# Fetching two feature rows per sample by DMA instead of turning them on TensorE, in a fused four-stage residual kernel

## The chip, the cores and the metric

The kernel runs on one core of a Trainium2 chip. The metric is the device time of one execution in microseconds (us), from three runs of the kernel before and, beside it, one execution taken with the hardware profiler. Engines are named as in the profile: PE is TensorE's matrix multiply, PEld its weight load, DVE is VectorE, ACT is ScalarE, POOL is GpSimd, SP is SyncE, which here only issues DMAs.

## What is computed

There are B = 128 samples, each a block of S = 128 positions by D = 512 features in float32. Four stages follow each other, and each adds its result to its input:

```
x1 = x  + pooled(softmax over a masked score, per sample one of three masks) / count
x2 = x1 + layernorm(x1 + relu(x1 @ W1[lang] + b1) @ W2[lang] + b2) * gamma[lang] + beta[lang]
x3 = x2 + zX * lap_x(x2) + zY * lap_y(x2) + zR * x2 * (1 - x2)
out = x3 + x3 @ W3[cat] + b3[cat]
```

`lap_x(y)` at a feature is left neighbour - 2y + right neighbour along the features; `lap_y` is the same along the positions. At both ends the neighbour is reflected: left of feature 0 stands feature 1, right of feature 511 stands feature 510. zX, zY and zR are one number per sample. `lang` picks one of 10 tables, `cat` one of 64 weight matrices of 512x512.

The change concerns the third stage and what it hands to the fourth.

## The kernel before

**Stages over iterations.** One sample takes several iterations of a software pipeline. `plan` is a hand-written list of (offset, function) pairs; iteration i runs through it and calls each function for sample i + offset. The order of the calls is the order of the instructions on every engine (`tc.manual_schedule()`), and no engine overtakes. The first iterations are written out one call at a time in `ramp`, up to about sample 4; after that the plain plan runs. Each iteration therefore does every stage once, for different samples, and its length is the time per sample.

**What stands where.** For sample b = i: scores and softmax (offset 0). Offset -1: the pooled sum, `pooled`, and the weight load `category` (one DMA of 1 MB, `w3_b`). Offset -2: the adapter's second product (`adapter`, L444), the layer norm (`statistics` on ACT, `deviation` on POOL, `centred` and `norm` on DVE), `edges` on ACT, which writes the two reflected columns 0 and 513 of the tile `y`, and `residual` on POOL (L597), which adds the identity matrix to `w3_b` so that the product gives x3 + x3 @ W. Offset -3: the diffusion stage. Offset -4: the product with `w3_b`, in three calls (`project_first`, `project_middle`, `project_last`, L604). Offset -5: `finish` on DVE (L618), which adds the bias row loaded by `category_row`, and `store`.

**The diffusion stage.** It is computed with features on partitions, since the product needs x3 transposed. `y_transpose` (L524) does four TensorE transposes of 128x128, each taking every fourth feature, so that partition p holds features 4p to 4p+3 as four planes of 128 positions. Neighbours along the positions are then neighbours in a plane. Neighbours along the features are the plane before and the plane after, except for a partition's first and last feature: their outer neighbours, 4p-1 and 4p+4, stand on partitions p-1 and p+1. The kernel before gets these two from two more transposes (L528, tile `tr_e`, called `outer`). `planes` copies all of it from PSUM to one tile of six planes, `yT`, on ACT: the four inner planes (L534), the two outer ones (L535) and the two reflected positions (L536). POOL then adds the neighbours: `ud` along the positions (L549), `lr` along the features (L557). ACT computes `own` (L541), a linear function of y, and DVE finishes in three steps: y * own (L564), + zY * ud (L568), + zX * lr (L575), which gives `x3T`. The first two write back to the PSUM tile `tr_y`.

**Buffers.** `tr_y` has one PSUM buffer; the small PSUM tiles (`zh`, `sc`, `pTp`, `h1` and `tr_e`) share four in turn. `yT` has two buffers, `w3` four, the bias and output rows (`b`) four.

**Queues.** All DMAs of the loop are issued by SP, in the order of the plan: `category` (L582, 1 MB), `store` (L621), `category_row` (L588), four DMAs of `load_blocks` (L98, 64 KB each, pieces of 512 bytes), `load_x` (L84). ACT issues DMAs only at the start. Every DMA reports its completion on one of eight semaphores, which the framework hands out; a DMA that is given a semaphore first waits until the DMA that had it before has landed.

**In one iteration** PE runs, in this order: `adapter`, the four transposes `tr_y`, the two `tr_e`, the transpose `pTp`, the first quarter of the product `po`, the transpose `sc`, `pooled` and `h`, the other three quarters of `po`, and `zh` (`first_products`, L330). ACT runs: `hidden` (tanh, L348, and a copy, L350), the copy of `pTp` (L415), `planes`, `statistics` (L476), `exps`, `own`, `bank_bias` (L317), the two copies of `pooled_copy` (L427, L431), `first_weights` (L310) and `edges` (L512). POOL runs: `mean`, `ud`, `deviation`, `lr`, `with_beta` (L436), `residual` (L597).

Of the kernel before, what the change touches and what calls it, by code (L numbers as in the profile page):

```python
# [22 lines left out]
def kernel(  # L23
# [37 lines left out]
    w3p = ctx.enter_context(tc.tile_pool(name="w3p", bufs=4))  # L61
    blocks = ctx.enter_context(tc.tile_pool(name="blocks", bufs=3))
# [3 lines left out]
    ps_tr = ctx.enter_context(tc.tile_pool(name="ps_tr", bufs=1, space=PSUM))  # L66
    ps_sm = ctx.enter_context(tc.tile_pool(name="ps_sm", bufs=4, space=PSUM))
# [10 lines left out]
    EARLY = 8  # L78
    R = 32
# [109 lines left out]
    mid = one.tile([P, NC, S], F32, tag="own", name="mid_tile")  # L189
# [324 lines left out]
    def y_transpose(b):  # L514

        s = st[b]  # L520
        yp = s["yp"]
        s["yT"] = ps_tr.tile([P, NC, S], F32, tag="tr", name=f"tr_y_{b}")
        for c in range(NC):
            nc.tensor.transpose(s["yT"][:, c, :], yp[:, c + 1 : c + 2 + D - NC : NC], ident)  # L524
        s["outer"] = ps_sm.tile([P, 2, S], F32, tag="sm", name=f"tr_e_{b}")

        for i, at in ((1, NC + 1), (0, 0)):
            nc.tensor.transpose(s["outer"][:, i, :], yp[:, at : at + D - NC + 1 : NC], ident)  # L528

    def planes(b):  # L530
        s = st[b]
        s["planes"] = two.tile([P, NC + 2, S + 2], F32, tag="yT", name=f"yT_{b}")
        inner = s["planes"][:, 1 : NC + 1, :]
        nc.scalar.copy(inner[:, :, 1 : S + 1], s["yT"])  # L534
        nc.scalar.copy(s["planes"][:, 0 : NC + 2 : NC + 1, 1 : S + 1], s["outer"])  # L535
        nc.scalar.copy(inner[:, :, 0 : S + 2 : S + 1], inner[:, :, 2 : S : S - 3])  # L536

    def own(b):
        s = st[b]
        s["own"] = one.tile([P, NC, S], F32, tag="own", name=f"own_{b}")  # L540
        nc.scalar.activation(  # L541
            s["own"], s["yT"], AF.Identity, bias=column(cy, b), scale=column(nzr, b)
# [19 lines left out]
    def diffuse_own(b):  # L562
        s = st[b]
        nc.vector.tensor_mul(s["yT"], s["own"], s["yT"])  # L564

    def diffuse_rows(b):
        s = st[b]
        nc.vector.scalar_tensor_tensor(  # L568
            s["yT"], s["ud"], column(zy, b), s["yT"], ALU.mult, ALU.add
        )  # L570

    def diffuse_columns(b):
# [3 lines left out]
            s["x3T"], s["lr"], column(zx, b), s["yT"], ALU.mult, ALU.add  # L576
# [43 lines left out]
    def store(b):  # L620
# [6 lines left out]
        (-1, category),  # L627
        (-2, adapter),
        (0, hidden_bias),
        (-5, finish),  # L630
        (-5, store),
# [7 lines left out]
        (-4, project_first),  # L639
        (-2, adapter_bias),  # L640
        (-2, mean),
        (-3, planes),
        (-3, neighbours),
# [8 lines left out]
        (-4, project_middle),  # L652
        (-3, own),
        (-3, side_neighbours),
        (1, bank_bias),
        (-1, pe_index),
        (-4, project_last),
        (0, shares),
        (-3, diffuse_own),
        (-2, norm),  # L660
        (0, weights),
        (-3, diffuse_rows),
# [4 lines left out]
        (2, first_weights),  # L667
        (-2, edges),
        (-3, diffuse_columns),
        (1, mask_at),  # L670
        (-1, with_beta),
        (-2, residual),
        (-3, category_row),
# [8 lines left out]
        act_index.6 first_products.0 fetch_ids.0 pe_index.0 load_w2.0 load_w2.2 first_products.1  # L682
        load_x.3 fetch_b1.0 row_at.0 hidden_bias.0 hidden.0 row_at.1 row_at.2 row_at.3
        row_by.vb.0 early_weights.3 row_by.vo.1 score.0 row_by.ab.2 turn_first.2 load_w2.4
        row_by.ab.3 load_w2.6 hidden_bias.1 mask_at.0 row_by.ab.5 masked.0 row_by.ao.4 load_w2.8
        scores.0 category.0 row_by.ab.6 mask_at.1 least.0 mask_at.2 mask_at.3 row_by.ab.8
        mask_at.5 row_by.vb.7 load_x.4 mask_at.4 row_by.ao.9 row_by.ab.10 row_by.ao.11
        row_by.ab.12 fetch_factors.0 row_by.ao.13 exps.0 row_by.ab.14 category.1 early_weights.4
        shares.0 weights.0 row_by.ao.15 mix_transpose.0 row_by.vb.16 hidden.1 row_by.vb.17
        mix_copy.0 pooled.0 score.1 masked.1 row_by.vs.20 scores.1 row_by.as.18 pooled_copy.0  # L690
        row_by.ao.19 first_products.2 least.1 residual.0 load_x.5 exps.1 hidden_bias.2
        turn_first.3 row_by.vo.21 row_by.as.22 row_by.vs.23 hidden.2 early_weights.5 adapter.0
        shares.1 row_by.ao.26 load_w1.0 row_by.as.24 adapter_bias.0 mean.0 row_by.vs.25
        weights.1 turn_first.4 factors.0 row_by.vo.29 mix_transpose.1 mix_copy.1 statistics.0
        row_by.as.28 pooled.1 residual.1 row_by.ao.27 score.2 load_x.6 first_products.3 masked.2
        pooled_copy.1 deviation.0 hidden_bias.3 category.2 load_w1.1 with_beta.0 centred.0
        early_weights.6 adapter.1 adapter_bias.1 mean.1 with_beta.1 hidden.3 turn_first.5 norm.0
        load_x.7 first_products.4 edges.0 scores.2 least.2 y_transpose.0 statistics.1 exps.2
# [62 lines left out]
```

## Time and profile before

| | |
|---|---|
| median of three runs | 1078.42 us (1077.36 to 1078.7) |
| the profiled execution's own time | 1078.29 us |
| its span in the trace | 1076.4 us |
| PE, DVE, POOL, ACT busy | 1053.2, 885.9, 775.9, 666.3 us |
| granted TensorE clock, mean | 0.994 |
| moved by DMA | 275.97 MB, 256 GB/s |

The page of the profile gives, in this order, the busy time of each engine, the span in 40 slices, the DMA queues, the chain of work that ended last (followed back from the last instruction), the costliest groups of instructions and the DMA issues with the median time from issue to landing. The timeline lists instructions with their start and length in us; "x4" means four in a row, merged. Matmul ends are modelled, so the time that a matmul takes on PE is best read as the distance to the start of the next one. A float32 matmul counts as two.

### The profile page before, as it was taken

What the parts mean: (1) busy time and instruction counts of PE and PEld (TensorE: products, weight loads), DVE (VectorE), ACT (ScalarE), POOL (GpSimd) and SP (SyncE); (2) the same over time, 40 slices, a digit from 0 to 9 for tenths busy, and PEclk for the clock granted to TensorE, in tenths of its full rate; (3) what the DMA queues carried; (4) which work ended last, traced back from release to release, by engine and by line L of the source; (5) the groups of instructions that cost most, each with busy time, mean ns of one, the idle gap of its engine ahead of it and who ended that gap; (6) DMA issues with size and microseconds to landing.
All of it is one profiled execution on the core that took longest, in us unless ns stands there. A gap on an engine that the chain in (4) does not pass through costs nothing.

```text
span 1076.4 us, 19485 instructions
## 1 busy us (share of the span) xinstructions
PE 1053.2 (98%) x3966; PEld 642.8 (60%) x3966; DVE 885.9 (82%) x2070; ACT 666.3 (62%) x2062; POOL 775.9 (72%) x921
## 2 busy tenths in 40 slices
PE   6889999999999999999999999999999999999997
PEld 4655665666666666666656656656656666566653
DVE  3578888888888888888888888888888888888885
ACT  4656666566566566666666666666665665665652
POOL 2557777777777777777777777777777777777775
PEclk8999999999999999999999999999999999999999
DMA  8789888787787877887788887887877887878853
GB/s 290 213 218 315 254 277 260 254 273 258 259 271 254 266 267 250 269 268 249 269 268 249 271 266 248 272 268 247 277 260 253 273 256 263 270 252 265 267 185 115
DMA packets 152646, 275.97 MB, mean 256 GB/s; under 512 B 16689, under 2 KB 84532, under 8 KB 136146
## 3 DMA queue, kind: packets, MB, share of 16 engines
q1 hardware_dynamic: 152326, 274.60, 78.3%
q8 instruction: 35, 0.57, 0.2%
q14 instruction: 81, 0.66, 0.2%
q10 hardware_dynamic: 204, 0.13, 0.1%
HBM read 241.11 MB, written 33.55 MB: 255 GB/s over the span
## 4 chain that ended last, share of the span: by engine, by line
PE 95%; DVE 2%; ACT 1%; issue 1%; DMA 0%; POOL 0%; SPq 0%; DVEq 0%; POOLq 0%; ACTq 0%
PE po L604 40%; PE zh L330 21%; PE pool L420 10%; PE pool L444 10%; PE tr_y L524 6%; PE tr_e L528 3%; PE h L422 3%; PE pTp L410 1%; PE sc L380 1%; PE row L274 0%; DVE tr_y L568 0%; DVE x3T L575 0%; DMA x<-in_x_dram 0%; PE tr_x L291 0%; ACT b_tab L277 0%
## 5 line engine op out<-in xcount | busy, mean ns | idle before, releaser
L604 PE MATMUL po<-w,x3T 128*128 128x512 f32 x1024 | 482.4, 594 | 1.3 <-issue 1.3
L604 PEld LDWEIGHTS po<-w,x3T 128*128 128x128 f32 x1024 | 175.3, 191 | 126.3 <-issue 126.3
L330 PEld LDWEIGHTS zh<-w,xT 128*128 128x128 f32 x1088 | 199.7, 193 | 78.7 <-issue 29.9
L330 PE MATMUL zh<-w,xT 128*128 128x256 f32 (+1 forms) x1088 | 244.4, 370 | 0.9 <-ACT yT L535 0.9
L597 POOL TENSOR_TENSOR w<-w,ident 128x512 f32<-128x512 f32 x128 | 198.3, 1549 | 10.8 <-DMA w<-in_L_cond_W_dram 10.8
L549 POOL TENSOR_TENSOR ud<-yT 128x512 f32<-128x512 f32 x128 | 133.0, 1039 | 100.9 <-ACT yT L536 100.9
L348 ACT ACTIVATE zh<-zh 128x128 f32<-128x128 f32 x128 | 33.6, 262 | 219.3 <-PE zh L330 207.9
L436 POOL TENSOR_TENSOR x<-x,beta_tab 128x512 f32<-128x512 f32 x128 | 162.9, 1273 | 4.5 <-ACT x L431 3.5
L557 POOL TENSOR_TENSOR lr<-yT 128x512 f32<-128x512 f32 x128 | 163.8, 1280 | 0.0
L469 POOL TENSOR_SCALAR mean<-total 128x1 f32<-128x1 f32 x128 | 28.4, 222 | 147.1 <-DVE pool L456 138.1
L420 PE MATMUL pool<-x,pT 128*128 128x512 f32 x256 | 132.7, 600 | 0.8 <-DVE gamma_tab L277 0.4
L444 PE MATMUL pool<-w_tab,h1s 128*128 x256 | 130.8, 593 | 0.0
L415 ACT COPY pT<-pTp 128x128 f32<-128x128 f32 x128 | 34.0, 266 | 143.2 <-PE pTp L410 143.2
L524 PEld LDWEIGHTS tr_y<-ident,y 128*128 128x128 f32 x512 | 80.9, 204 | 66.2 <-issue 62.2
L494 DVE SCALAR_TENSOR_TENSOR pool<-pool,mean,gamma_tab 128x512 f32<-128x512 f32 x128 | 97.0, 758 | 25.4 <-ACT y L476 24.9
L385 DVE TENSOR_REDUCE least<-sc 128x1 f32<-128x128 f32 x128 | 37.3, 292 | 90.4 <-PE sc L380 90.4
L575 DVE SCALAR_TENSOR_TENSOR x3T<-lr,zx,tr_y 128x512 f32<-128x512 f32 x128 | 95.6, 747 | 13.5 <-DVE tr_y L568 0.5
L541 ACT ACTIVATE own<-tr_y,cy,nzr 128x512 f32<-128x512 f32 x128 | 99.1, 774 | 0.0
L618 DVE TENSOR_TENSOR b<-po,b 128x512 f32<-128x512 f32 x128 | 88.5, 691 | 11.8 <-PE po L604 3.8
L568 DVE SCALAR_TENSOR_TENSOR tr_y<-ud,zy,tr_y 128x512 f32<-128x512 f32 x128 | 95.7, 748 | 0.1
L506 DVE SCALAR_TENSOR_TENSOR y<-pool,rstd,x 128x512 f32<-128x512 f32 x128 | 95.7, 747 | 0.0
L456 DVE SCALAR_TENSOR_TENSOR pool<-pool,b_tab 128x512 f32<-128x512 f32 x128 | 88.7, 693 | 2.2 <-PE pool L444 2.0
(82 smaller groups left out, 1649.9 us busy)
## 6 DMA issues: line engine op xcount, KB each, us to landing
w<-in_L_cond_W_dram SPq DMA_DIRECT2D x128, 1024.0 KB, 5.2
x<-in_x_dram SPq DMA_DIRECT2D x128, 256.0 KB, 3.5
b<-in_L_cond_b_dram SPq DMA_DIRECT2D x128, 256.0 KB, 4.0
out_dram<-b SPq DMA_DIRECT2D x128, 256.0 KB, 2.8
blocks<-in_x_dram SPq DMA_DIRECT2D x480, 64.0 KB, 4.0
w_tab<-in_L_cond_W_dram SPq DMA_DIRECT2D x5, 512.0 KB, 5.6
w_tab<-in_L_cond_W_dram SPq DMA_DIRECT2D x16, 160.0 KB, 6.3
w<-in_L_cond_W_dram SPq DMA_DIRECT2D x9, 256.0 KB, 3.8
```

Of the source, the lines that this page charges most:

```text
L330: nc.tensor.matmul(s["zh"][:, part, :], s["xT"][:, c, :], w[:, c], start=(c == 0 and b < EARLY), stop=(c == NC - 1), skip_group_check=True,)
L420: nc.tensor.matmul(s["xx"], s["pT"], xt[b], start=True, stop=True)
L436: nc.gpsimd.tensor_add(s["x1"], s["x1"], beta_tab[:, ds(at, D)])
L444: nc.tensor.matmul(s["xx"], s["h1"], w2_tab[:, ds(s["pe_at"], D)], start=False, stop=True, skip_group_check=True,)
L494: nc.vector.scalar_tensor_tensor(s["xx"], s["xx"], s["mean"], gamma_tab[:, ds(s["dve_at"], D)], ALU.subtract, ALU.mult,)
L506: nc.vector.scalar_tensor_tensor(s["yp"][:, 1 : D + 1], s["xx"], s["rstd"], s["x1"], ALU.mult, ALU.add)
L524: nc.tensor.transpose(s["yT"][:, c, :], yp[:, c + 1 : c + 2 + D - NC : NC], ident)
L541: nc.scalar.activation(s["own"], s["yT"], AF.Identity, bias=column(cy, b), scale=column(nzr, b))
L549: nc.gpsimd.tensor_add(s["ud"], planes[:, 1 : NC + 1, 0:S], planes[:, 1 : NC + 1, 2 : S + 2])
L557: nc.gpsimd.tensor_add(s["lr"], planes[:, 0:NC, 1 : S + 1], planes[:, 2 : NC + 2, 1 : S + 1])
L597: nc.gpsimd.tensor_add(diag, diag, ident.unsqueeze(1).to_broadcast([P, NC, P]))
L604: nc.tensor.matmul(s["po"], s["x3T"][:, c, :], w3t[b][:, c, :], start=(c == 0), stop=(c == NC - 1))
```

## The change

The two transposes `tr_e` go, except for the first two and the last two samples. Instead, one tile `yT` holds the six planes of two samples. The outer planes are filled by four DMAs for each pair of samples, issued on ScalarE's queue after the planes of the second sample are there: plane 4 of partition p goes to plane 0 of partition p+1, and plane 1 of partition p+1 to plane 5 of partition p. Each of the two copies is split into 112 partitions and 15. The two reflected features are copied by ACT. Since the DMAs take time, `neighbours`, `side_neighbours`, `own` and the three steps of `diffuse` move from offset -3 to -5, the product from -4 to -6, `finish` and `store` from -5 to -7; `category` moves from -1 to -4, `residual` from -2 to -5 and ahead of `with_beta`, `category_row` from -3 to -5. The sum of the diffusion gets a PSUM tile of its own, `tr_s`, instead of writing over `tr_y`; `own` reads `yT` in SBUF instead of `tr_y` in PSUM. Buffers change: `w3` 4 to 3, the blocks of x for two samples in one tile with 2 buffers instead of 3, large transposes in PSUM 1 to 2, small PSUM tiles 4 to 3. `load_blocks` loads two samples with the same number of DMAs, every second iteration. `ramp` is reordered in places.

```diff
-    w3p = ctx.enter_context(tc.tile_pool(name="w3p", bufs=4))
-    blocks = ctx.enter_context(tc.tile_pool(name="blocks", bufs=3))
+    w3p = ctx.enter_context(tc.tile_pool(name="w3p", bufs=3))
+    blocks = ctx.enter_context(tc.tile_pool(name="blocks", bufs=2))
...
-    ps_tr = ctx.enter_context(tc.tile_pool(name="ps_tr", bufs=1, space=PSUM))
-    ps_sm = ctx.enter_context(tc.tile_pool(name="ps_sm", bufs=4, space=PSUM))
+    ps_tr = ctx.enter_context(tc.tile_pool(name="ps_tr", bufs=2, space=PSUM))
+    ps_sm = ctx.enter_context(tc.tile_pool(name="ps_sm", bufs=3, space=PSUM))
...
+    def turned_beside(b):
+        return b < 2 or b >= B - 2
...
     def load_blocks(b):
-        if b < EARLY:
+        if b < EARLY or b % 2:
             return
-        st[b]["blocks"] = blocks.tile([P, D], F32, tag="blocks", name=f"blocks_{b}")
+        both = blocks.tile([P, 2, D], F32, tag="blocks", name=f"blocks_{b}")
+        for i in range(2):
+            st[b + i]["blocks"] = both[:, i, :]
         for q in range(Q):
             nc.sync.dma_start(
-                st[b]["blocks"][q * R : (q + 1) * R, :].rearrange("r (i e) -> r i e", i=Q),
-                x[b, :, q * P : (q + 1) * P].rearrange("(i r) e -> r i e", r=R),
+                both[q * R : (q + 1) * R, :, :].rearrange("r b (i e) -> r b i e", i=Q),
+                x[b : b + 2, :, q * P : (q + 1) * P].rearrange("b (i r) e -> r b i e", r=R),
             )
...
+        if not turned_beside(b):
+            return
         s["outer"] = ps_sm.tile([P, 2, S], F32, tag="sm", name=f"tr_e_{b}")
...
     def planes(b):
         s = st[b]
-        s["planes"] = two.tile([P, NC + 2, S + 2], F32, tag="yT", name=f"yT_{b}")
+        if b % 2 == 0:
+            both = two.tile([P, 2, NC + 2, S + 2], F32, tag="yT", name=f"yT_{b}")
+            for i in range(2):
+                st[b + i]["planes"] = both[:, i, :, :]
+            st[b + 1]["both"] = both
         inner = s["planes"][:, 1 : NC + 1, :]
         nc.scalar.copy(inner[:, :, 1 : S + 1], s["yT"])
-        nc.scalar.copy(s["planes"][:, 0 : NC + 2 : NC + 1, 1 : S + 1], s["outer"])
+        if turned_beside(b):
+            nc.scalar.copy(s["planes"][:, 0 : NC + 2 : NC + 1, 1 : S + 1], s["outer"])
+        else:
+            nc.scalar.copy(s["planes"][0:1, 0, 1 : S + 1], s["yT"][0:1, 1, :])
+            nc.scalar.copy(
+                s["planes"][P - R : P, NC + 1, 1 : S + 1], s["yT"][P - R : P, NC - 2, :]
+            )
         nc.scalar.copy(inner[:, :, 0 : S + 2 : S + 1], inner[:, :, 2 : S : S - 3])

+    def fetch_beside(b):
+        if turned_beside(b) or b % 2 == 0:
+            return
+        both = st[b]["both"][:, :, :, 1 : S + 1]
+        for a, e in ((0, P - 16), (P - 16, P - 1)):
+            nc.scalar.dma_start(both[a + 1 : e + 1, :, 0, :], both[a:e, :, NC, :])
+            nc.scalar.dma_start(both[a:e, :, NC + 1, :], both[a + 1 : e + 1, :, 1, :])
+
     def own(b):
         s = st[b]
-        s["own"] = one.tile([P, NC, S], F32, tag="own", name=f"own_{b}")
+        s["sum"] = ps_tr.tile([P, NC, S], F32, tag="tr", name=f"tr_s_{b}")
         nc.scalar.activation(
-            s["own"], s["yT"], AF.Identity, bias=column(cy, b), scale=column(nzr, b)
+            s["sum"],
+            s["planes"][:, 1 : NC + 1, 1 : S + 1],
+            AF.Identity,
+            bias=column(cy, b),
+            scale=column(nzr, b),
         )
...
     def diffuse_own(b):
         s = st[b]
-        nc.vector.tensor_mul(s["yT"], s["own"], s["yT"])
+        y = s["planes"][:, 1 : NC + 1, 1 : S + 1]
+        nc.vector.tensor_mul(s["sum"], s["sum"], y)
```

In the plan, `planes` now comes before the first quarter of the product and `neighbours` after it; `fetch_beside` (offset -3) stands between `first_weights` and `edges`; `residual` stands between `diffuse_columns` and `with_beta`. In the changed kernel's sources the new DMAs are on lines L565 and L566, the weight load on L617, the bias row on L623, `store` on L656, `lr` on L591, `residual` on L632.

More of the change, by code (lines that the diff above doesn't have):

```diff
@@ L687 @@
[L687 to L698, printed above, removed]
@@ new lines @@
+        mix_copy.1 statistics.0 row_by.as.28 row_by.ao.27 pooled.1 residual.1 score.2 load_x.6
+        first_products.3 masked.2 pooled_copy.1 deviation.0 hidden_bias.3 category.2 with_beta.0
+        centred.0 early_weights.6 adapter.1 adapter_bias.1 mean.1 with_beta.1 hidden.3
+        turn_first.5 norm.0 load_x.7 first_products.4 edges.0 scores.2 least.2 y_transpose.0
+        statistics.1 deviation.1 exps.2 shares.2 weights.2 first_products.5 mix_transpose.2
+        planes.0 score.3 centred.1 masked.3 neighbours.0 own.0 norm.1 scores.3 early_weights.7
@@ L710 @@
+        pooled_copy.3 project_last.0 least.4 norm.2 exps.4 with_beta.3 edges.2 residual.2
+        diffuse_rows.1 load_w1.10 category_row.1 load_w1.6 shares.4 load_w1.5 load_w1.8
+        weights.4 load_w1.9 diffuse_columns.1 load_w1.11 load_w1.12 load_w1.4 load_w1.13
+        load_w1.14 load_w1.15
     """
```

74 lines of the change are left out of this document (39 added, 35 removed).

## The prediction

> **What bounds the kernel now.** I read the page's first part, then its chain of waits, then the timeline of two iterations in the middle, then the time that DMAs take to land.
>
> ```profile
> PE 1053.2 (98%) x3966; PEld 642.8 (60%) x3966; DVE 885.9 (82%) x2070; ACT 666.3 (62%) x2062; POOL 775.9 (72%) x921
> ...
> PE 95%; DVE 2%; ACT 1%; issue 1%; DMA 0%; POOL 0%; SPq 0%; DVEq 0%; POOLq 0%; ACTq 0%
> PE po L604 40%; PE zh L330 21%; PE pool L420 10%; PE pool L444 10%; PE tr_y L524 6%; PE tr_e L528 3%; PE h L422 3%; PE pTp L410 1%; PE sc L380 1%; PE row L274 0%; DVE tr_y L568 0%; DVE x3T L575 0%; DMA x<-in_x_dram 0%; PE tr_x L291 0%; ACT b_tab L277 0%
> ```
>
> PE is busy for 98% of the span, and 95% of the chain that sets the end is PE. `tr_e`, which the change removes, holds 3% of it, about 32 us. The timeline says what one `tr_e` is worth and how far the other engines are from being the bound:
>
> ```profile
> 604.95 1.28 POOL L557 TENSOR_TENSOR lr<-yT 128x512 f32<-128x512 f32 x1
> ...
> 605.55 0.65 ACT L310 COPY w<-w_tab 128x512 f32 x1
> ...
> 606.07 0.22 ACT L512 COPY y<-y 128x2 f32<-128x2 f32 x1
> ...
> 607.83 1.02 PE L444 MATMUL pool<-w_tab,h1s 128*128 x2
> 608.03 0.26 ACT L348 ACTIVATE zh<-zh 128x128 f32<-128x128 f32 x1 [1.74 <-PE zh L330]
> 608.22 0.69 DVE L618 TENSOR_TENSOR b<-po,b 128x512 f32<-128x512 f32 x1 [0.41 <-PE zh L330]
> 608.26 0.20 PEld L524 LDWEIGHTS tr_y<-ident,y 128*128 128x128 f32 x1 [0.24 <-issue]
> ...
> 609.15 0.41 PE L528 MATMUL tr_e<-ident,y 128*128 128x128 f32 x2
> ...
> 609.40 0.27 PE L410 MATMUL pTp<-ident,q 128*128 128x128 f32 x1
> ...
> 610.37 0.27 PE L380 MATMUL sc<-ident,masked 128*128 128x128 f32 x1
> ```
>
> The adapter's product starts at 599.79, 607.83 and 615.86: an iteration is 8.03 us, and no PE row in it has an idle time before it that matters. The two `tr_e` start at 609.15 and the next transpose at 609.40; over all iterations this distance is 0.243 us in the middle. By busy time DVE has 885.9/128 = 6.9 us of work in an iteration, POOL 6.1, ACT 5.2.
>
> **What goes.** 124 samples lose `tr_e`: 124 x 0.243 = 30.1 us, if PE stays the bound at 8.03 - 0.24 = 7.79 us. This is the only thing that the change takes off the path.
>
> **What is swapped at no cost, and its cover.** ACT loses the outer copy (L535, 0.39) and gets two copies of 128 elements; by the nearest row (L350, 0.27 for 128x128) that is +0.15 at most, -0.1 if they overlap as neighbouring rows do. ACT waits 1.7 + 1.1 us per iteration for PE (L348, L415). `own` reads SBUF and writes PSUM instead of the reverse: copies of 256 elements take 386 ns one way (L317) and 393 ns the other (L535), so nothing, bound +-0.05. The product y * own on DVE has the same sizes (L564, 677 ns); if it rises to the 758 ns of L494, +0.08 against DVE's 0.9 us of idle time per iteration. POOL's instructions are the same; `ud` no longer waits for ACT (0.8 us in each iteration) and fills the gap before `mean`. The transpose `tr_y` no longer waits for `x3T`. With three small PSUM buffers for four tiles, each is reused after its reader is done by the order of the engines. Without these covers ACT's 0.15 would come once per iteration: 19 us.
>
> **What is added: four DMAs per pair.** The trace of before has no DMA inside SBUF, so its terms are bounded by rows. Load first: per sample 254 pieces of 512 bytes. The trace's 67,843 packets of 512 bytes took 31 ns in the mean: 254 x 31 / 16 engines = 0.49 us. All packets now take 78.3% of 8.03 = 6.29 us per iteration, so 6.78 of 7.79, 87%. By bytes alone (+6%) it would be 86%, by the mean packet of all sizes (+21% of packets) 98%. I take 87%.
>
> Issue time: SP's DMAs take 0.34 to 0.49 us each, ACT's four at the start 0.30 to 0.59. Four come to 1.4 to 2.4 us on ACT in every second iteration, I take 1.7. They stand after L310 (start 5.76 us into an iteration, 5.5 in the shorter one; at the start of the trace ACT's DMA issue of 0.59 us runs beside the table load, so it need not wait for the copy's end), so from 5.6 to 7.3. Behind them in ACT's order wait `edges` (L512, 0.22) and then `hidden`. PE's `tr_y` waits for `edges`: its weight load is due at 608.26, that is 8.47 into an iteration, 8.23 in the shorter one, with 0.2 us to spare. 7.3 + 0.22 = 7.5 fits; at 2.4 us of issue it is 8.2 and still fits. `hidden` waits for `zh` until 8.0 anyway.
>
> Landing time L of the fetch is the open price, because more waits for it than `lr`. In the changed program's instruction order the DMAs of ScalarE take four of the eight completion semaphores. From about sample 16 on, in iterations that fetch, SP's weight load is given the semaphore of the fetch's first DMA, and the bias row, the load of x and the next weight load those of the other three. So SP stands still until the fetch has landed, then issues two 1 MB loads close together. SP now issues the weights at 606.39, before the iteration that they belong to; after the change, from the start of the fetching iteration, at 5.6 + L + 0.1. What needs them:
>
> ```profile
> w<-in_L_cond_W_dram SPq DMA_DIRECT2D x128, 1024.0 KB, 5.2
> x<-in_x_dram SPq DMA_DIRECT2D x128, 256.0 KB, 3.5
> b<-in_L_cond_b_dram SPq DMA_DIRECT2D x128, 256.0 KB, 4.0
> out_dram<-b SPq DMA_DIRECT2D x128, 256.0 KB, 2.8
> blocks<-in_x_dram SPq DMA_DIRECT2D x480, 64.0 KB, 4.0
> ```
>
> - The weights land at 5.7 + L + 5.2 = 10.9 + L. `residual` (1.55 us) must follow and end before the sample's first quarter of `po`, at 2 x 7.79 + 1.44 = 17.0. So L up to 4.5.
> - The bias row lands after the weights and one store. Now a row issued at 601.09 lands 4.0 later, 1.4 us after the weights issued at 598.35 (5.3). So 12.3 + L. `finish` (L618) waits for it at 15.6. Behind `finish` on DVE stand the score and the mask, and PE's `sc` waits for the mask; in the timeline the mask is ready 0.8 us before `sc` starts (609.50 against 610.37). So DVE is late from L = 3.3 on, PE from 4.0 on.
> - `lr` itself: all four have landed at 7.3 + L, and the first sample's `lr` comes at about 7.79 + 4.7 = 12.5. So L up to 5.2.
>
> So PE loses nothing up to L = 4.0, and L - 4.0 per pair above it, 62 times. The rows for L: store 2.8 (minimum 2.0), load of x 3.5 (2.9), blocks 4.0 (2.8), all with other transfers of SP's queue ahead of them, up to the weights' 5.2. The fetch has ACT's queue for itself, and SP's is nearly empty while SP waits; it starts in SBUF as the store does and has the blocks' piece size. I take 3.0, between the store's median and the load's, and keep 2.0 and 5.2 as ends.
>
> [...]
>
> **Ends.** The two more iterations cost at the end and save at the start. At the end, after the last `with_beta`, POOL has three more diffusions with `residual` than PE needs for anything else: 1.04 + 1.27 + 1.55, some 3.7 us apart, against PE's 3.6 for a `po`. From the last `with_beta` (1055.6) to the end are now 20.8 us; I count 1.3 + 4.8 + 3 x 3.7 + 3.7 (`po`) + 0.7 (`finish`) + 2.8 (store) + 1.0 of waits = 25.4, +4.6. At the start, iterations 5 and 6 lose a `po` each (3.44 us by starts); PE is busy 10.9 of 12.7 and 8.8 of 9.5 us there, so 2 to 6.9 us come back. Together -2 to +3; I take +1.
>
> **Sum.** Against the profiled execution's own 1078.29 us, 0.1 under the median of 1078.42 and 1.9 above its span: 1078.3 - 30.1 + 1 = **1049 us**. With L up to 4.0 and the ends' bounds: 1046 to 1051, and 1043 to 1058 with 0.1 us of small waits per pair or a few more us won at the end.
>
> **Rivals.**
> 1. *Slower: the semaphores chain SP to the fetch.* If L is above 4.0, PE pays (L - 4.0) x 62. It outweighs the 30 us from L = 4.5; at 5.2, the weights' own landing, 74 us: 1123. For it: blocks, with the same pieces, have a median of 4.0 and a maximum of 7.6, and DMA is at 87%, with two weight loads in a burst; the blocks and x of the iteration before may still be in flight. Against it: these rows queue behind SP's weights, the fetch does not.
> 2. *The gain is eaten in part.* ACT's issues take longer than at the start. With 0.73 us each, as one small load at the start took on SP, they end at 8.5, `edges` at 8.7, PE 0.3 us late per pair: 19 us, 1068. The same size comes from L = 4.3. For it: DMA issues on ACT are shown only on an idle chip. Against it: SP's are mostly 0.34 to 0.49.
> 3. *No change: another engine binds at 8 us.* DVE at 6.9 of 7.79 has the least room; it would need 1.1 us more per iteration, and its added work is 0.08. More likely L near 4.5, where loss and gain cancel: 1078.
>
> **Chances.** Forecast 0.62, rival 2 0.13, rival 3 0.06, rival 1 0.19. About 0.2% (2 us) is what a measurement of this kernel can tell from no change. Faster: 0.75, same 0.06, slower 0.19. The range goes from 1043 to 1077 and leaves out rival 1, of 0.19; the likeliest case alone has 1043 to 1058.
>
> **What would show it.** Right: adapter starts 7.79 us apart; no `tr_e` between `tr_y` and `pTp`; the fetch's issue at about 5.6, of 1.7 us; landing at 3; the weight loads in pairs, the first right after the fetch lands; `residual` and `finish` with waits under 1 us; no wait of `tr_y` for `edges`. Wrong: iterations that alternate, with PE's `sc` waiting for the mask or `po` for POOL (L too long, rival 1), or `tr_y` waiting for ACT (rival 2). The forecast fails if the fetch lands after more than 4 us, or if the second of two weight loads is late as well, which I placed at 3 us after the first with half an iteration to spare.

## The result, and the profile after

The changed kernel takes 1116.05 us (median of four runs), the kernel before 1078.56 us beside it on the same chip: a ratio of 1.033, with an interval of 1.027 to 1.040. It is slower. The forecast was 1049 us; what happened is the first rival, which its own price put at 1123 us. The profiled execution took 1111.7 us, its span is 1109.8 us, the granted clock 0.987. Runs of one kernel below can differ by up to 3%; the ratios leave out those over 1.5% above the fastest, the medians do not, and where the profiled run is one that is left out (e4, e7, e14) its waits are read and not its length.

The first part of the page, and its list of DMA issues (the last column is the median time from issue to landing, over those DMAs whose landing the trace ties to their issue):

```profile
PE 1045.1 (94%) x3718; PEld 610.8 (55%) x3718; DVE 899.9 (81%) x2071; ACT 696.8 (63%) x2185; POOL 769.7 (69%) x921
...
w<-in_L_cond_W_dram SPq DMA_DIRECT2D x128, 1024.0 KB, 6.0
x<-in_x_dram SPq DMA_DIRECT2D x128, 256.0 KB, 4.7
b<-in_L_cond_b_dram SPq DMA_DIRECT2D x128, 256.0 KB, 7.1
out_dram<-b SPq DMA_DIRECT2D x128, 256.0 KB, 4.1
blocks<-in_x_dram SPq DMA_DIRECT2D x240, 128.0 KB, 5.8
yT<-yT ACTq DMA_DIRECT2D x124, 112.0 KB, 3.7
```

PE is busy for 94% instead of 98%: it waits. Every transfer of SP lands later than before, the bias row 7.1 us after its issue instead of 4.0. Some of these medians rest on few DMAs: that of the store on 9 of 128, and on 6 of 128 before. The updates of the semaphores (16 for each DMA) give every landing of the middle of the run, and by them the store took 7.0 us instead of 3.7, the weights 7.0 instead of 5.2, the bias row 7.4 instead of 4.1.

**Iterations alternate.** From adapter start to adapter start, the iteration in which a fetch is issued takes 8.55 us in the mean, the one between 7.85. Three of four short ones are 7.79; the long ones lose their time at their start, by what the fetch of the pair before made late. Cut at the adapter of sample 20 and the last one, the span before is 198.0 + 857.4 + 21.0 us, after 201.2 + 877.2 + 31.5. The middle lost 19.7 us where 26.0 were to be won (107 iterations of 0.243), and the end lost 10.4.

**What PE waits for.** In the middle PE loses 43.8 us, 30.6 of them ahead of the first quarter of `po`. The page's groups name two reasons (the last column is the idle time of the engine just before these instructions, and what ended most of it):

```profile
L639 PE MATMUL po<-w,x3T 128*128 128x512 f32 x1024 | 488.2, 600 | 32.0 <-POOL w L632 10.9
...
L632 POOL TENSOR_TENSOR w<-w,ident 128x512 f32<-128x512 f32 x128 | 197.0, 1539 | 64.0 <-DMA w<-in_L_cond_W_dram 45.4
...
L653 DVE TENSOR_TENSOR b<-po,b 128x512 f32<-128x512 f32 x128 | 88.5, 692 | 60.0 <-DMA b<-in_L_cond_b_dram 36.0
```

The page puts `po` down to `residual` (L632), the last name it finds. I compared, for each sample, when `residual`, `x3T` and the `finish` of the sample before were done: at all 34 late quarters up to sample 121 `finish` (L653) ended last, and `po` has one PSUM buffer, so it must wait for it. `finish` itself waited 36 us in all for the bias row. This is the first rival's chain, with a shorter last link. One stretch of the timeline, with one of the longer landings of the fetch, has it whole ("ACTq" and "SPq" are issues of DMAs):

```profile
601.89 0.70 ACTq L565 DMA_DIRECT2D yT<-yT  x1
...
602.63 0.63 ACTq L566 DMA_DIRECT2D yT<-yT  x1
...
603.30 1.39 ACTq L565 DMA_DIRECT2D yT<-yT  x1
...
605.09 0.92 ACTq L566 DMA_DIRECT2D yT<-yT  x1
...
607.80 0.36 SPq L617 DMA_DIRECT2D w<-in_L_cond_W_dram  x1
...
608.82 0.34 SPq L623 DMA_DIRECT2D b<-in_L_cond_b_dram  x1
...
610.76 0.34 SPq L617 DMA_DIRECT2D w<-in_L_cond_W_dram  x1
...
613.96 1.54 POOL L632 TENSOR_TENSOR w<-w,ident 128x512 f32<-128x512 f32 x1 [2.27 <-PE zh L338]
...
615.84 0.69 DVE L653 TENSOR_TENSOR b<-po,b 128x512 f32<-128x512 f32 x1 [1.54 <-DMA b<-in_L_cond_b_dram]
...
616.63 1.10 PE L639 MATMUL po<-w,x3T 128*128 128x512 f32 x2 [1.37 <-issue]
```

Read it from the top. The four issues take 0.70, 0.63, 1.39 and 0.92 us on ACT. The first fetch lands at 607.44, 5.6 us after its issue; SP, which needs its semaphore, issues the weights at 607.80. The weights land at 613.8 and `residual` starts at once; the bias row, issued at 608.82, lands at 615.75, and `finish` starts at 615.84, 1.54 us late. PE's `po` follows 1.37 us late. What SP waits for, over the whole span (us in total, times, longest), first before, then after:

```profile
SPq L621 <- DVE b L618: 213.8, 116, 5.9
SPq L582 <- PE po L604: 192.2, 118, 3.7
...
SPq L106 <- DMA out_dram<-b: 295.4, 82, 6.7
SPq L617 <- DMA yT<-yT: 82.7, 53, 4.8
SPq L106 <- DMA b<-in_L_cond_b_dram: 40.5, 54, 4.2
```

Before the change SP's long waits were for PE and DVE, that is for buffers to come free. Now it waits for landings: 83 us for the fetch ahead of the weights, and much more, 295 us at the loads of the blocks, for its own store issued just ahead. With four of eight semaphores at the fetch, SP's own DMAs come round to the same semaphore sooner.

### The profile page after: what moved, and what is told of

Read it like the earlier page. It is cut to its first block, busy times and chain, and to the rows that moved or that the text cites. A ratio compares the mean times of both kernels' runs of the same rounds, so it can differ in the third digit from the quotient of the medians.

```text
span 1109.8 us, 19207 instructions
## 1 busy us (share of the span) xinstructions
PE 1045.1 (94%) x3718; PEld 610.8 (55%) x3718; DVE 899.9 (81%) x2071; ACT 696.8 (63%) x2185; POOL 769.7 (69%) x921
## 3 DMA queue, kind: packets, MB, share of 16 engines
q1 hardware_dynamic: 148486, 274.59, 79.4%
## 5 line engine op out<-in xcount | busy, mean ns | idle before, releaser
L639 PE MATMUL po<-w,x3T 128*128 128x512 f32 x1024 | 488.2, 600 | 32.0 <-POOL w L632 10.9
L632 POOL TENSOR_TENSOR w<-w,ident 128x512 f32<-128x512 f32 x128 | 197.0, 1539 | 64.0 <-DMA w<-in_L_cond_W_dram 45.4
L591 POOL TENSOR_TENSOR lr<-yT 128x512 f32<-128x512 f32 x128 | 163.5, 1277 | 30.3 <-DMA yT<-yT 19.9
L653 DVE TENSOR_TENSOR b<-po,b 128x512 f32<-128x512 f32 x128 | 88.5, 692 | 60.0 <-DMA b<-in_L_cond_b_dram 36.0
L532 PEld LDWEIGHTS tr_y<-ident,y 128*128 128x128 f32 x512 | 78.0, 205 | 75.3 <-ACT y L520 45.2
L484 ACT ACTIVATE y<-pool,total 128x512 f32<-128x512 f32 x128 | 88.2, 689 | 37.0 <-DVE pool L464 34.6
L520 ACT COPY y<-y 128x2 f32<-128x2 f32 x128 | 25.9, 202 | 135.7 <-DVE x3T L610 96.4
L610 DVE SCALAR_TENSOR_TENSOR x3T<-lr,zx,tr_s 128x512 f32<-128x512 f32 x128 | 95.6, 747 | 18.8 <-POOL lr L591 5.6
L571 ACT ACTIVATE tr_s<-yT,cy,nzr 128x512 f32<-128x512 f32 x128 | 99.8, 780 | 1.9 <-DVE x3T L610 1.8
L497 POOL TENSOR_SCALAR ve<-squares 128x1 f32<-128x1 f32 x128 | 24.4, 190 | 107.3 <-ACT y L484 107.0
L603 DVE SCALAR_TENSOR_TENSOR tr_s<-ud,zy,tr_s 128x512 f32<-128x512 f32 x128 | 95.7, 747 | 0.3
```

The lines of the kernel that those rows point to most:

```text
L571: nc.scalar.activation(s["sum"], s["planes"][:, 1 : NC + 1, 1 : S + 1], AF.Identity, bias=column(cy, b), scale=column(nzr, b),)
L591: nc.gpsimd.tensor_add(s["lr"], planes[:, 0:NC, 1 : S + 1], planes[:, 2 : NC + 2, 1 : S + 1])
L603: nc.vector.scalar_tensor_tensor(s["sum"], s["ud"], column(zy, b), s["sum"], ALU.mult, ALU.add)
L610: nc.vector.scalar_tensor_tensor(s["x3T"], s["lr"], column(zx, b), s["sum"], ALU.mult, ALU.add)
L632: nc.gpsimd.tensor_add(diag, diag, ident.unsqueeze(1).to_broadcast([P, NC, P]))
L639: nc.tensor.matmul(s["po"], s["x3T"][:, c, :], w3t[b][:, c, :], start=(c == 0), stop=(c == NC - 1))
```

## The experiments

Theory A: SP's queue is in order, and waits for landings (the fetch's, and its own DMAs' that share what semaphores are left) take away the lead of the weights and the bias row. Rival B: the issue time on ACT. Rival C: the bytes of the fetch in full DMA engines. Rival D: `lr`, which waits for the fetch. All are against the kernel before on the same chip (1078.0 to 1079.4 us).

**e1: the bias row one iteration earlier.**

```diff
-        (-5, category_row),
+        (-4, category_row),
```

> The bias row is loaded one iteration earlier (category_row at offset -4 instead of -5); all else as in the changed kernel. Theory A (in pairs of iterations, SP's loads stand behind the fetch's completion semaphores, and the bias row of the odd sample lands too late for finish, which holds back the first quarter of the next product: 31.8 us of PE time in the trace of the changed kernel): this wait goes, the time falls by 20 to 32 us, to 1080 to 1092, and the rest of the loss (start, end, late weights) stays. Theory B (ScalarE's DMA issues, 3.6 us in every second iteration, hold edges and with them PE): nothing changes, 1111 to 1120. Theory C (the 16 DMA engines are full, every load is late): the wait only moves to residual, less than 10 us are won, 1105 or more.

1099.03 us, ratio 1.018 [1.015, 1.021]: 17 us back, A half right. `finish` no longer waits for the row; all 28 late quarters of `po` now wait for `residual`, 22.8 us, and that for the weights.

**e2: no fetch at all.** The outer planes are filled by ACT from the kernel's own inner planes, so the sums along the features are those of other neighbours at a partition's first and last feature.

```diff
-            nc.scalar.copy(s["planes"][0:1, 0, 1 : S + 1], s["yT"][0:1, 1, :])
...
+            nc.scalar.copy(s["planes"][:, 0 : NC + 2 : NC + 1, 1 : S + 1], s["yT"][:, 0 : NC : NC - 1, :])
...
-        (-3, fetch_beside),
```

> The four DMAs of a pair are left out; ACT copies two inner planes to the places of the outer ones, so the sums along the features are wrong for a partition's first and last feature. The move of the diffusion by two iterations, the buffers and the paired loads stay. If the DMAs cause the loss (theories A, B and C alike): iterations of 7.79 us throughout, 1050 plus what start and end cost, 1050 to 1060. If the move, the buffers or the paired loads of x cause part of it: 1065 or more.

1055.87 us, ratio 0.980 [0.978, 0.981], all iterations 7.79 us. The fetch costs 60 us. SP waits for buffers only.

**e3: the move alone.** Every sample keeps the two `tr_e`, no fetch.

```diff
-        return b < 2 or b >= B - 2
+        return True
```

> All samples keep the two transposes, no fetch; the move by two iterations, the buffers and the paired loads stay. The gain and the DMAs are both out, so what is left over 1078 is the price of the move: theories A, B and C give 1078 to 1086 (start and end only); if the move itself hurts in the middle, more than 1090.

1086.4 us, ratio 1.007 [1.005, 1.009]; iterations of 8.04 us as before; start 1.4 us shorter, end 9.6 longer. So the move by two iterations, with its buffers and paired loads, costs 7.7 us, and dropping `tr_e` gains 30.5 (e3 less e2).

**e4: the four DMAs on SP's queue.**

```diff
-            nc.scalar.dma_start(both[a + 1 : e + 1, :, 0, :], both[a:e, :, NC, :])
+            nc.sync.dma_start(both[a + 1 : e + 1, :, 0, :], both[a:e, :, NC, :])
```

> The same four DMAs of a pair, issued by SP instead of ScalarE. ACT is free of 3.6 us of issues per pair, SP gets them in its order behind store. Theory B: the loss of PE behind edges goes, the time falls, but by the trace this loss is only 2 us in the middle and 8 at the start. Theory A: SP now also waits for the planes themselves, but its loads no longer stand behind a whole fetch in the same way; the bias row follows the fetch in SP's order, so it stays late: 1090 to 1120. Theory C: no change, 1110 or more.

1084.32 us over nine runs (1073 to 1103), ratio 1.003 [1.000, 1.005]. About 32 us come back, but runs differ by 3%. `lr` now waits for the fetch, 80 us in 39 iterations of the profiled run.

**e5 and e6: other DMAs in the way.** The blocks are loaded in the other kind of iteration; by the built program the fetch's semaphores then go back to a store, a bias row and two blocks, and no longer to the weights. e6 adds e1's edit.

```diff
-        (3, load_blocks),
+        (4, load_blocks),
...
-        load_w1.14 load_w1.15
+        load_w1.14 load_w1.15 load_blocks.8
```

> The four loads of blocks are moved by one iteration, so that all eight other DMAs of a pair still stand in the same queue, but the completion semaphores of the four fetches now return to a store, a bias row and two loads of blocks; both weight loads get the semaphore of the weight load before. Theory A (SP stands still behind the fetch, so weights and bias row come late): the weights no longer wait, but one bias row of two still does, so between a third and two thirds of the 60 us that the fetch costs come back: 1075 to 1095 us, and the pTp to po loss falls from 30 to under 15 us. Rival C (the fetch fills the DMA engines, whatever the order): 1110 to 1120, as after. Rival B (the 3.6 us of issue on ScalarE): also 1110 to 1120.

> As the run before, and the bias row is issued one iteration earlier in the plan as well, so that neither weights nor bias row have to land within an iteration after the fetch. Theory A: nearly all of the loss but the ends comes back, 1058 to 1072 us, with odd and even iterations both under 7.9 us. Rival B or C: 1095 to 1105, no better than the early bias row alone had.

1116.62 us, 1.035 [1.028, 1.042], and 1101.04 us, 1.019 [1.016, 1.021]: no better than the changed kernel and e1. A in the narrow form, weights and fetch on one semaphore, fell. SP's waits in e5 show why:

```profile
SPq L656 <- DMA yT<-yT: 163.0, 55, 6.6
SPq L617 <- DMA w<-in_L_cond_W_dram: 130.8, 55, 4.3
SPq L623 <- DMA yT<-yT: 67.9, 31, 7.1
```

The wait for the fetch has moved to the store (L656) and the bias row, and as SP is in order the weights behind them wait too. By this run alone B and C were as good as A.

**e7: an eighth of the bytes.** Outer planes as in e2, then DMAs of 16 of the 128 positions (so the sums at the edges hold for those only); issues, semaphores and order unchanged.

```diff
-        both = st[b]["both"][:, :, :, 1 : S + 1]
+        both = st[b]["both"][:, :, :, 1:17]
```

> The outer planes are filled by ScalarE copies of the kernel's own inner planes, and the four DMAs then move only 16 of the 128 positions (pieces of 64 bytes instead of 512), so that the sums at the first and last feature of a partition are right for those positions alone. Issues, their number, semaphores and order stay as in the changed kernel; the bytes fall to an eighth. Theory A and rival B: the chain stays and a fetch still takes 3 us or more, 1095 to 1118. Rival C (traffic): most of the 60 us goes, 1055 to 1070.

1100.33 us over ten runs, ratio 1.010 [1.005, 1.015] (some 1089 us by the ratio, which rests on two of the ten runs). Seven eighths of the bytes are worth 16 to 27 us of 60; the median landing fell from 3.7 to 2.9 us. SP still waits 111 us for the fetch and 260 for its stores. Against C, if not alone enough.

**e8: the four DMAs on GpSimd's queue**, full bytes. In the built program their semaphores are not those of SP's DMAs.

```diff
-            nc.scalar.dma_start(both[a + 1 : e + 1, :, 0, :], both[a:e, :, NC, :])
+            nc.gpsimd.dma_start(both[a + 1 : e + 1, :, 0, :], both[a:e, :, NC, :])
```

> The same four DMAs, issued by GpSimd instead of ScalarE. In the built program their completion semaphores then are not those that SP's loads use, ScalarE is rid of 3.6 us of issue per pair, and the bytes are the same. Theory A (SP stands still behind the fetch): SP's waits on the fetch are gone, weights and bias row go out where they do without a fetch, and the time is 1058 to 1075 us, unless GpSimd's issues take more than its 1.7 us of room in an iteration, which would show as late residuals. Rival C (traffic): 1085 to 1115 with GpSimd in time. The run with an eighth of the bytes gave back about 16 us, which is what traffic can be worth by it.

1122.37 us, 1.041 [1.039, 1.043]: the total missed A's range, and the trace says where. The iteration with the fetch is 7.80 us, the other 8.85. Issue times of SP, counted from the adapter start of the fetching iteration (middle of the run, 10% to 90%):

| | no fetch (e2) | after | GpSimd (e8) |
|---|---|---|---|
| bias rows | 1.3, 9.1 | 9.3 to 15.8, both | 1.3, 9.6 |
| weights | 6.4, 14.1 | 7.6 to 15.3 | 6.4, 15.2 |

With the fetch off SP's semaphores, SP is regular to 0.1 us or so, in the middle no `residual` waits for its weights, and the iteration that shares the DMA engines with the fetch has its 7.8 us. The 1.06 us of the other iteration are GpSimd's own:

```profile
606.03 0.77 POOL L565 DMA_DIRECT2D yT<-yT  x1
...
606.80 0.68 POOL L566 DMA_DIRECT2D yT<-yT  x1
...
607.48 0.59 POOL L565 DMA_DIRECT2D yT<-yT  x1
...
608.07 0.58 POOL L566 DMA_DIRECT2D yT<-yT  x1
...
608.66 1.55 POOL L632 TENSOR_TENSOR w<-w,ident 128x512 f32<-128x512 f32 x1
...
610.26 1.12 PE L639 MATMUL po<-w,x3T 128*128 128x512 f32 x2 [0.80 <-POOL w L632]
```

2.62 us of issue stand ahead of `residual`, and `po` waits for it, in all 54 late cases of the middle.

**e9: the fetch to a tile that nothing reads**, outer planes as in e2. Only `lr`'s wait goes.

```diff
+        side = one.tile([P, 2, 2, S], F32, tag="side", name=f"side_{b}")
-            nc.scalar.dma_start(both[a + 1 : e + 1, :, 0, :], both[a:e, :, NC, :])
+            nc.scalar.dma_start(side[a + 1 : e + 1, :, 0, :], both[a:e, :, NC, :])
```

> The outer planes are filled by ScalarE copies of inner planes (sums along the features wrong at a partition's first and last feature), and the four DMAs of unchanged size go to a tile that nothing reads. Issues, semaphores and bytes stay; only GpSimd's wait for the fetch goes. Theory A: no change from the changed kernel, 1100 to 1118. Rival D (the sum of side neighbours that waits for the fetch, 20 us of GpSimd's idle time, makes residual and the products late): 1055 to 1085.

1121.19 us, 1.039 [1.032, 1.046]. D falls: `lr` costs nothing on ACT's queue.

**e10: as e9, one partition per DMA (1 KB).**

```diff
-        for a, e in ((0, P - 16), (P - 16, P - 1)):
+        for a, e in ((0, 1), (1, 2)):
```

> As the run before, but each of the four DMAs moves one partition (1 KB), so that bytes are next to nothing and the issues and the landing are as short as they get; the semaphores are shared as in the changed kernel. Theory A: the chain stays, but by the landing of 2 to 2.5 us instead of 3.3 to 5.5 it asks little; 1056 to 1080. If the shared semaphores cost at any landing time, 1090 to 1110.

1077.82 us, 0.997 [0.995, 0.999]. With next to no bytes, no reader and a landing of 1.9 to 2.6 us (medians of the four, by their semaphores), four DMAs per pair still cost 22 us against e2, by the same signs: in the middle 14.1 of PE's loss stand ahead of `po`, `finish` waits for the row, and SP waits 347 us for its stores at the blocks. So sharing the semaphores cost 22 us here even at this landing time, and 60 with the full fetch, which landed after 3.3 to 4.4 us (medians of the four). On ACT the issues still take 1.08, 0.57, 0.56 and 0.56 us, and PE's `tr_y` lost nothing in the middle: B is at most small here.

**e11: two DMAs of 127 partitions on GpSimd**, one right after `mean`, where GpSimd is idle.

```diff
+        nc.gpsimd.dma_start(both[1:P, :, 0, :], both[0 : P - 1, :, NC, :])
...
+        nc.gpsimd.dma_start(both[0 : P - 1, :, NC + 1, :], both[1:P, :, 1, :])
```

> Two DMAs instead of four, each over 127 partitions, issued by GpSimd: the one for the left places right after the mean, where GpSimd waits 1.07 us for ScalarE's statistics, the one for the right places where the four stood. In the run with four on GpSimd, only the iteration after a fetch was long (8.85 us), by GpSimd's 2.6 us of issue ahead of the residual; the residual had some 1.57 us of room. Two issues take an estimated 0.8 us each (0.77 and 0.59 for 112 and 15 partitions), one in idle time and one within the room. Theory A: 7.79 to 7.85 us in both iterations, 1055 to 1064 us, faster than the kernel before. Rival C (traffic), or a landing over 6 us in one larger DMA that makes the side neighbours late: 1075 to 1110.

1877.37 us, 1.738 [1.729, 1.746]. Nothing of what was expected. The queue's line in e11 (packets, MB, share) and its landing:

```profile
q0 software_dynamic: 65472, 18.02, 6.8%
...
yT<-yT POOLq DMA_DIRECT2D x124, 127.0 KB, 17.2
```

In e8 the same rows were 9920 packets and 5.6 us. The run has 74,354 packets under 512 bytes, 57,660 more than the changed kernel, one issue takes 3.68 us, and `lr` waits 564 us. The split into 112 and 15 partitions is not an ornament: with it GpSimd's queue gave 1122.37 us in e8 and, with the large ones at the same early place, 1126.99 in e12.

**e12: 112 and 15 again on GpSimd**, the two large ones (`fetch_most`) right after `mean`, the small ones (`fetch_last`) where all four stood.

```diff
         (-2, mean),
+        (-3, fetch_most),
...
-        (-3, fetch_beside),
+        (-3, fetch_last),
```

> The four DMAs of 112 and 15 partitions again, on GpSimd's queue. The two large ones are issued right after the mean, where GpSimd otherwise waits 1.07 us for the statistics; the two small ones stay ahead of the residual. By the rows of the run with all four on GpSimd: 0.77 and 0.68 us for the large ones, 0.59 and 0.58 for the small ones, 2.62 in all, less 0.9 of idle time after the copy of the planes, so the residual is 1.7 us later than without a fetch, with 1.57 us of room: 0.15 us of loss per pair at the most, some 10 us, against 1.06 us per pair with all four ahead of the residual. Theory A: 1055 to 1070 us, faster than the kernel before; SP's issue times as regular as without a fetch. Rival C (traffic) or a late sum of side neighbours: 1085 to 1120.

1126.99 us, 1.046 [1.044, 1.048]: 7.79 and 8.91 us, missed. The idle time was smaller than I had put it: the first issue waits for ACT's last copy of the planes and starts 0.51 us after `mean`, so `residual` came only some 0.45 us earlier than in e8, against the adapter's start. And a new wait took the rest:

```profile
608.68 1.55 POOL L637 TENSOR_TENSOR w<-w,ident 128x512 f32<-128x512 f32 x1
...
609.85 1.70 DVE L381 TENSOR_SCALAR masked<-masks,score 128x128 f32 x1
...
610.17 1.27 POOL L444 TENSOR_TENSOR x<-x,beta_tab 128x512 f32<-128x512 f32 x1
...
611.59 0.14 PEld L388 LDWEIGHTS sc<-ident,masked 128*128 128x128 f32 x1 [1.01 <-DVE masked L381]
```

The mask took 1.70 us, where it takes 0.29 in the kernel before and about 0.6 in e2; it ends 0.1 us after GpSimd's second instruction, and 60 of the 128 masks took over 1 us. All 60 end about 0.1 us after the second of two instructions of GpSimd that follow each other. What holds VectorE that long, no run shows.

**e13: the large ones ahead of `residual`, the small ones behind it.**

```diff
         (-5, residual),
+        (-3, fetch_last),
```

> The four DMAs on GpSimd's queue once more, the two large ones ahead of the residual as in the run with all four there, the two small ones after it. The large ones are 0.77 and 0.68 us, so the residual is 1.45 us later than without a fetch, with 1.57 us of room by the run with four. The small ones then land some 3 to 4.9 us after 609.0 us in the scale of that run's timeline, against 612.7 to 613.5 us for the sum of side neighbours that needs them. Theory A (only the loads' order, or on GpSimd its issue time, costs; the bytes do not): odd iterations fall from 8.85 to between 7.8 and 8.1 us, even ones stay below 8.0: 1056 to 1076 us, faster than the kernel before. If the bytes or the landing decide: odd or even iterations over 8.3, 1090 to 1125.

1115.38 us, 1.035 [1.033, 1.037]. The iteration that e8 had at 8.85 is 7.83, as expected, but the other, 7.80 there, is 8.68: the small DMAs, 4 to 5 us to landing, come too late for the next `lr`, which waits 76.5 us in 61 iterations. The profile puts 46.6 of these down to the loads of blocks, which `lr` doesn't read; in all 61 it starts 0.2 us (once 0.5) after the last of the four DMAs has landed. Behind it `residual` and, on DVE, `x3T` and `finish` are late. GpSimd's room in a pair is less than 2.6 us.

**e14: e4 and e1 together.**

```diff
-            nc.scalar.dma_start(both[a + 1 : e + 1, :, 0, :], both[a:e, :, NC, :])
+            nc.sync.dma_start(both[a + 1 : e + 1, :, 0, :], both[a:e, :, NC, :])
...
-        (-5, category_row),
+        (-4, category_row),
```

> The four DMAs on SP's queue, where 23 of the 30 us that the products lost in the profiled run came from a late bias row, and the bias row issued one iteration earlier in the plan, which was worth 17 us on ScalarE's queue. If the late bias row is what is left: 1062 to 1076 us, faster than the kernel before. If the fetch is then late itself, since it stands behind SP's own waits (GpSimd waited 80 us for it in that profiled run): 1078 to 1100.

1090.59 us over ten runs (1079 to 1098), 1.008 [1.005, 1.011], no better than e4. On SP's queue the row was not the cause: `lr` waits 79 us for a fetch that SP issues late, and DVE's `finish` stands behind the `x3T` that waits for `lr`.

**What is settled.** Against e2 the changed kernel's span is 56 us longer: 8.8 at the start, 45.8 in the middle, 1.7 at the end. The middle's part comes from SP's lost lead: e8 and e12 keep the bytes and free SP's semaphores, and the late loads are gone; e10 keeps the semaphores without the bytes, and they are back. The landing times say the same (medians of the middle in us, by the semaphores' updates):

| | before | no fetch (e2) | after | 1 KB (e10) | GpSimd (e12) |
|---|---|---|---|---|---|
| weights | 5.2 | 5.1 | 7.0 | 7.4 | 5.2 |
| bias row | 4.1 | 4.1 | 7.4 | 8.2 | 4.3 |
| store | 3.7 | 3.6 | 7.0 | 7.6 | 3.5 |

With the full bytes of the fetch and SP regular (e12) SP's transfers land as without a fetch; with next to no bytes and the semaphores shared (e10) they land late. So it is not the bytes of the fetch that make them late. What after and e10 have in common is that SP, once let go, sends its transfers close together: the two weight loads of a pair go out 4.0 and 3.7 us apart in the median, instead of 7.8 in e2. C as a cost of its own is not seen: the fetch's bytes act through its own landing (e7: 2.9 us with an eighth of them, 3.7 with all). D is excluded by e9 for ACT's queue. B is 1.7 us at `tr_y` in the middle and 3.0 at one place of the start; the rest of the start's part was not followed up. No placement was found in which the fetch fits: on GpSimd it delays `residual`, on SP it is late itself. Weights with four buffers instead of three, which might give the lead back, were not tried. What stays open is how the middle's 46 us divide between waits for the fetch and SP's waits for its own store. No version that computes the whole result is faster than the kernel before.

## Why the prediction was wrong

- **Removal of `tr_e`, 30.1 us: right.** The undisturbed iteration is 7.79 us, and e3 less e2 is 30.5.
- **Swaps at no cost: right in sum.** e2, with all of them, holds 7.79 in every iteration. In detail the mask on DVE doubled from 0.29 to 0.6 us, which I had not looked for: `ud` on POOL now runs beside it, and the mask ends 0.1 us after `ud`. DVE's idle time hid it.
- **Load of DMA, 87%: the share fits (79.4% for SP's queue and 6.0% for ACT's), and it was not the bound.**
- **Issue on ACT, 1.7 us, bound 2.4: more than twice as long.** Measured 3.6 to 3.7. The small DMAs of 15 partitions took longest (1.38 and 0.92 against 0.68 and 0.64). They begin 4.5 us into the iteration or somewhat later, instead of at 5.6, and end 0.4 us after the next adapter's start in the median; `edges` then takes 0.2, and PE's `tr_y` is due 0.86 after that start. So `tr_y` lost 1.7 us in the middle; at the start it lost 8.0 in one place, where e2, without a fetch, has 5.0. The second rival's mechanism thus cost little.
- **Landing L = 3.0: somewhat low, and not what decided.** In the middle the first DMA of the fetch landed after 3.3 us in the median and 3.6 in the mean, the others after 4.0, 4.0 and 4.4. Only in 12 of 52 pairs was the first over 4.0; the stretch shown, with 5.6, is one of them. The lowest row that was weighed, 2.8 for the store, was a median of 6 stores of 128, and all stores of the middle took 3.7; the load of x, 3.5, was the nearest row. The argument that "the fetch has ACT's queue for itself, and SP's is nearly empty" failed too: SP's bursts of two weights, two rows, stores and blocks are still landing when the next fetch goes out: in the middle 2 to 5 of SP's DMAs were still to land at the first issue of a fetch, 4 in the median.
- **The step that failed: "The bias row lands after the weights and one store", 1.4 us after the weights, "So 12.3 + L".** Counted from the first issue of the fetch that is 6.7 + L, 9.7 us at L = 3. Over the 52 pairs of the middle it was 11.9 in the mean: 0.6 too many are L, 0.2 the time from the fetch's landing to the issue of the weights, 1.1 the weights' own landing (6.3 instead of 5.2) and 0.3 the row behind them. The prediction moved only L; the 5.2 was taken from the kernel before, where SP's loads go out evenly, and it is the term that was mis-sized most. So "PE loses nothing up to L = 4.0" was false: in 32 of the 52 pairs the quarter of `po` behind the row was late, and in 21 of these L was 4.0 or less. In the stretch shown it is 615.75 - 601.89 = 13.9, and of the 4.2 too many 2.6 are L.
- **The path from `finish` to PE: shorter than forecast.** The prediction led it over the score, the mask and PE's `sc`. In the trace the first quarter of `po`, which stands ahead of `sc`, waits for `finish` itself. That DVE is late first and PE next held.
- **What the sum left out: SP's waits for its own landings.** It counted the four semaphores as a wait for the fetch. They also leave SP four fewer to go round, and it stood 295 us at the blocks for a store issued just ahead. e10 puts a price on the sharing: 22 us with a fetch that lands after 1.9 to 2.6 us, where the sum has nothing.
- **Ends, +1: wrong.** The end cost 10.4 us instead of 4.6, and e3 and e2 have 9.6 and 8.8 without any fetch, so it is the move, not the fetch. From the last `with_beta` to the end the trace has 30.2 us instead of the 25.4 that were counted: POOL's last `residual` ends 2.7 us later than by the count, and what follows it takes 2.1 more. The start won 5.5 us in e2, as forecast, and lost it to the first fetches (+3.2).
- **First rival, 0.19: it happened, but not by its own condition.** SP chained to the fetch, late weights and rows, and the place of the loss were as it said. Its condition, L over 4, was met in 12 of 52 pairs, and its price of (L - 4.0) x 62 was not what the runs measured: the pairs cost 0.81 us in the mean, 50 us over 62 pairs, at a landing of 3.3 in the median. That its 1123 us lie near the measured 1116 is luck: it took L = 5.2 for every pair.

## What to carry to other kernels

A DMA that replaces work on the bounding engine has to be counted in the queue that its completion semaphore touches, and not only in its own: write down, for every later DMA, whose landing it now waits for, and how many semaphores are left to the rest. Where a prediction hangs on a landing time, take it from transfers in the same traffic as the new one will meet, look on how many of them the median rests, and ask whether the change bunches the loads that were there already: here their own landing times moved more (the weights' from 5.2 to 7.0 us, the bias row's from 4.1 to 7.4) than the new one was off (3.3 instead of 3.0). An engine with idle time in the mean may have none at the place where the issue has to stand: GpSimd was busy for 72% before, and 2.62 us of issue ahead of `residual` made every second iteration 1.06 us longer (e8).

## What the runs showed of the hardware

- The issue of the fetch's four DMAs took 0.68 and 0.64 us for 112 partitions and 1.38 and 0.92 for 15 on ACT (medians of the middle), 0.77 and 0.68, then 0.59 and 0.58, for the same four on GpSimd (e8, the stretch shown), and 1.08, 0.57, 0.56 and 0.56 for one partition each on ACT (e10).
- Two DMAs of 127 partitions on GpSimd's queue came to 65,472 packets over the run and landed after 17.2 us (e11), where the four of 112 and 15 came to 9920 and landed after 5.6 (e8). Other loads were slower with them: the weights landed after 10.5 us, by the same list that gives 6.0 for the changed kernel.
- One VectorE instruction of 128x128 took 0.29 us with GpSimd idle beside it (before), about 0.6 beside one GpSimd instruction (e2) and 1.70 beside two in a row (e12); in e2 and e12 it ended 0.1 us after GpSimd's.
- The same 1 MB load landed after 5.2 us (median of the middle, before and e12) where SP's loads went out evenly, and after 7.0 (after) and 7.4 (e10) where they went out in bursts, though the kernel before and e10 both moved 256 GB/s in the mean.
